# A kernel whose instructions are queued by a 12,085-letter string: the same letters in another order

## The chip, the cores and the metric

The kernel runs on one core of a Trainium2 chip. A core has five instruction queues that run side by side, each in its own order: TensorE (PE, matrix products; the loading of its weights is shown apart as PEld), VectorE (DVE), ScalarE (ACT), GpSimd (POOL) and SyncE (SP, which here only starts DMA transfers). Work on one queue waits for work on another through semaphores. The metric is the device time of one execution in microseconds (us); lower is better.

## The reference, cut to what matters

The input is x, 8 images of 56 x 56 positions with 128 channels, all in float32. Two layers follow one another.

```
# layer 0, per image
xp     = x @ w_in + b_in
h      = gelu(batchnorm(depthwise_conv3x3(x)))
offset = h @ w_off + b_off                   # 4 groups x 9 points x 2
mask   = softmax(h @ w_msk + b_msk)          # over the 9 points
y      = sum over points of mask * bilinear(xp at point + offset) @ w_out + b_out
x      = x + gamma1 * layernorm(y)
x      = x + gamma2 * layernorm(gelu(x @ w_fc1 + b_fc1) @ w_fc2 + b_fc2)
# layer 1, t = x as 3136 tokens per image
n      = layernorm(t)
q, k, v = n @ Wq, n @ Wk, n @ Wv
t      = t + softmax(causal(q @ k.T / sqrt(3136))) @ v
probs  = softmax(layernorm(t) @ gate_w.T + gate_b, over tokens)
# each of 64 experts takes its 8 likeliest tokens of each image,
# pools them by probs, applies a two-layer gelu network,
# and adds the result back to those tokens, weighted by probs
```

## The kernel before, in words

An image is cut into four groups of 448 or 896 tokens (image 0: 448, 896, 896, 896; the others: 896, 896, 896, 448), 32 groups (b, s) in all; a group is worked in tiles of 128 tokens. The bilinear sampling is done as 25 fixed taps around each position: the weights of the taps are computed from the offsets and the mask, a 5 x 5 neighbourhood of each token is gathered from DRAM, multiplied by the weights and added up.

The work of a group is split over twenty Python generators. Each has a letter:

| letter | generator, line | what one group does there | steps in the string |
|---|---|---|---|
| b, k | bring, back | start the loads of x, and of x turned channel-first (xT), on SP | 54, 56 |
| p | prepare L509 | turn x on PE, multiply by w_in (L538), copy into xg, whose edge columns POOL clears (L495), and store the image for the gather | 280 |
| v | conv L562 | depthwise conv, DVE (L576), and its gelu, ACT | 560 |
| c | plan L590 | offsets and mask on PE (L601); softmax and tap weights on DVE (L621, L645, L648), ACT and POOL (L653 to L669) | 912 |
| f | fetch L680 | start the gather of g, 1600 KB per tile, on SP (L691) | 200 |
| g | weigh L696 | copy the weights (ACT, L706), multiply g by them (DVE, L715, 3.5 us a tile) | 256 |
| s | sums L723 | fold the 25 taps on POOL (L732; the first fold of a tile takes 3.5 us), the rest on PE (L747, L749) | 1475 |
| m | project | w_out, layernorm, fc1 (PE L856), gelu (ACT L863), fc2 (PE L877), layernorm | 1432 |
| n | norm L957 | layernorm, and q, k, v on PE | 800 |
| q | scores | q times k on PE (L1066) | 776 |
| x | maxes | scores to SBUF with the row maximum, DVE (L1092, L1108) | 972 |
| e | exps | exp, ACT (L1140) | 776 |
| t, u | turn, pour | transpose the weights on PE (L1158), copy them out of PSUM on ACT (L1173) | 776, 776 |
| a | attend | weights times v on PE (L1203) | 776 |
| y | mix | divide by the row sum and add to t, DVE (L1235) | 102 |
| o | after L1250 | layernorm, gate, and per pair of images the choice of the top 8 tokens (DVE L1344 to L1404, POOL gathers) | 1008 |
| h, w | share L1495, settle | pooling for the experts; derived weights | 82, 16 |

A generator yields before each instruction or small bundle of instructions; up to the next yield is one step. The order in which the steps of all generators are issued is not planned while the kernel is built: it is written out as the string `ORDER` (lines 109 to 242), and the main loop (about line 1754) goes through it letter by letter:

```python
with tc.manual_schedule(engines=engines):
    for line in ORDER:
        if lines["project"].at == len(groups) and not experts:
            give_up()
        lines[NAMES[line]].step()
```

Each letter takes its generator one step on. So the order within a generator is fixed, and the string decides how the twenty are interleaved; that sets the order of the instructions in each of the five queues. An instruction whose data are late holds up everything behind it in its queue. In what follows a step is named by letter, group and count: c(6,1).13 is the fourteenth step of plan for image 6, group 1.

Buffers limit how far one generator may run ahead of another. `rings` counts them: five PSUM banks for general use ("gen"), three gather buffers g, eight score rows S, three q, two xT, two z, one accumulator av. A step that takes a buffer is only written where the string has already given one back. Line 1617 (`class Line`) holds the step; the rules on which group may begin stand from line 1665 on, for instance that project of group n needs sums of group n to be done and after of group n - 4.

ACT holds one table of functions at a time, and changes between gelu and exp need a table load. The load stands where the string puts a gelu step behind an exp step or the other way round.

When the string is used up, a fixed phase for the experts follows (about lines 1765 to 2085); it is the same in both kernels.

Of the kernel before, what the change touches and what calls it, by code (L numbers as in the profile page):

```python
# [79 lines left out]
def need(engine, us, take=None, give=None, since=None, kind=None, when=None, lock=False, also=None):  # L80
# [29 lines left out]
    "ppppbpppppppwbpwwpppwvvfvvvvvvvvbppwcpccccckpwcccpccpccpbpppwfccwvccvccvccvvvccvwwcccvfvcgvg"  # L110
    "vvvvvwvvswsvvgsvcpcccfccspcbppcsppgccccwpcpwcscppvgcsvcvvvvvvcccvfwcvsccbcvcvsvvcvcvscvscsfk"
    "wmvvgvmmmcgcmpbcsfsgpmcvscmccvvcpvsmcsgmsvsmvmvmmmscvcbsmfmpmgfmgmcvsfscgmmmmmmmsnnfnsppnnpn"
    "gccnnsngncnnvnnvsnsvccnqsscvxscfcvpqfcppcevcvxqvscxevcvcqevcksxbpctcecctcmppucmumcpagtpcmgpa"
    "mmuapctbuycgfcpmccbacpmpmscyvoscmcmvmossmmmmcccvcmmsmgmmfvmmsmmsvmvgmommscvmomvcgcmsovscmmmv"
    "fgvmmsfmvmmsovmfovmvvccmomsvgmvmmmmmoosvmncconnsnvpspcnnopnnosogfncskccnnncnsoopnpkponnncpcs"
    "ncgnsnnmcnmgpqqmncxpxmqfsfmxpmnnqmcmgcmmmcxmccmmvmmmxmmmssnmvngvxmmmqnmmqcmsvxxeeqbmxxcmsvee"
    "mmtuvmqmevvqcaxcxvstfxmmgqcmmvvmvuvmmtcvcmcmsxetcbumqgmvufsavtssxmmgcxmmsvqueqmemmnnxcanoste"
    "auqecvtnaunnnsxatfesnngnunncnyqtsnsvunanxxntenqfsaxeouocgcnxstgusqtfnengvkxnaxspuefqssxsstqs"
    "etpemmasnuamqpusftgxxmsqansmxqxpstsassqmuafengeempxusxmysmsqvmvmsmnvatxevssnuvfmqgnsgtxmssaa"
    "vmsmmuvytssugxssmqvtmxtmakaemmmcmmusceesumcmmsssqcesqocqxmxfssstaxkmbauomtssvmtvumqmmcsaxgqu"  # L120
    "mfaqetcxxoaeutecusctqvgsscxsvaumxsqvsaefocqvcosmmvmsxvxmoommtuscsxqtavmqessovmuxsxetmqesemxc"
    "taoumvasqtsymuqmfmcvuxccxapsetnsnxaqetxmcuqcpvatvqmexxxcotcvumanenceotevqnucmxuncvapcbncecpe"
    "ommupepncapqmmpamcgxctnvvpmvvocfpcmmvumomngmsttsnpnsgacmcmnupaqcoxtmbqsmsxeqpmxuucnccxmosacn"
    "oanskntstuapommncsmspsnpesmmsnunmestapgocmucaecpnontsoycsummpnsfoaqqexoqxnomacecncmmoxmssmto"
    "mqstgmmsouxqumqotmfoxgmxmmubxseqoeoxnqsaacgasscepyonteooqutesoousskqotccesuafoomtxqcxxcmxmoo"
    "mmqmmtuoomxooaaxsusqoaatexeosqoeusttesonucosqseqogxxxaukeatvutqxqunatcstxucfxsnsvgssscooaoeu"
    "ennnsaqqasxxtaqsutnexastueoovvsqesqecsfxngutxoqxfoattavxussqqsguesauteevutasuntasxqonsoexqns"
    "smeytsveuaxuctxsqgacmqnuxsqamstnxxmxaeussfmmssssveeaetngmnfqstumamvmssamsvxmuensnmqmtggsxqqm"
    "acnxsfmexssmmtoesstusmsscmgmsnnuqsxmsatmuuatscccqnvuxqanxmfqxnsmemsnemsnecxavcttmsmguvsqcqas"
    "xeantmktbexsmuvvnasuamccuvsneaotevmufvsmmcmvtqusssfacsxmvcgmtmpsmcmqucscsmxqspqscxcqspamaxxe"  # L130
    "mesfctepemmmquxtsectqutxymxeaeeesmuuamctepcqasqtcumcssmaxxqumcgmptutakaapnnnnnnnmunnmtexgpmy"
    "onnmupmpoqtatnnmxabuoufvgxmssvecccqxconnayqnonnosmstxetvecosunnauncssoxtgcmcscsusconqosaasxv"
    "ocncossmocnqaoqxxqxxceqooonxxtcoesunqovqoxaooxxsotsoencsoseoyftnoueccvessqccecvvtamouooeuavf"
    "ctocyoxtmoammqmuouoovtommocueqgvmoaxmxxoatqmmmomxccceaevooooqmxquvmmtooquovtoxxvcmmvuvsmcaet"
    "moxmgomsoossmmomovvmkomovugomoqmmssosxomeqsxqsfmcxmmsesammeptmccmxnbnnnnnettacnpsesecumuamnc"
    "cnftpunsceqatugxqmqcyqnxasacpsxnumxsnqstqscuxtnpsensanquagsvmssencsaxxxncemttnuancssvcutmvne"
    "snqvuxcvsqnfcmscnatsmaxmscgqvasxcxqvemeeusgstuvfassnvvxsmmnasgsstvmfytutcqmmauvxqkquvvevmsxx"
    "vssevatucnentamsuegtqbaxvoxtyqvcusxeqqxmoomaaxecsotvpocxtmuoqecsucqooesomfcaxxauoptmessscmqm"
    "umptgoofeonoatcssuusoopcanatcsxpneoconqnqupvxnxsgotsxaaoesevccspusvtqasuegacteonqsqnuxtcofnx"
    "nuaqsnssofsosevvvnmtxtsxvbgomqubuamsxoxssmqxeaomsqmxtomeummpsmcatsgesssuqsvqevmxqmssepxscyms"  # L140
    "mmctmmamssvaxqtnmfmpcsgsxqsxnummumtmaeumckcmfmtsessqesacxtcsuacaetpusxqqctuneoagxqamscpuasxg"
    "txqpnueqcxtmxetecpumscueaastmfoxstseqceemfmstcpxasqumcosmmumxaguqqqxmcstmsxxxsmteqcmucxessaa"
    "ussstgcqxcecqstfmauxeaeemccycsqmugctxpsssmcacoqustgcaxqccuxmtquasmtcsmmxsxqpmmuseaskeaatexcq"
    "synsoootfcnsooepoonsqutexaopnotuupxsqavoxqetosseuocnnnnunmomxmtssfgqoaquoxsnxanxtsecbqavnteu"
    "oqscexvevutoataamsstvuoeefauvqxegvnoqcqsxxmcutvmasomxussmqtnsnucaoboascmvfvxqvsgtxvmxoesusga"
    "oqmxsomstfemvogmovtosumqsmexmconnussqoemtvsqcessxskasuatsnxmmnxanmxugefasstxnunasxmvmnmmqsex"
    "sovmxemsnmsmtvsnqcutfnsecunamagqxmemsvcxamyssvmmmccccstmsmgsctmsungmsmsmqmqtmecuxcssqefcaxxm"
    "cmtutamugxemcamsqsmkcuteayeqxmuyeysoooposnstooeucmnntnaxsocmspxnooaoononquapocooncxeynpnotco"
    "sfmcqtncuamtnmnxeuoonnacnmnsncmocsunnfkxnsonongoomqmmoaqqnnxeomoxtoqnsoomogpmmunxoonmxooqpmm"
    "sqxmopcstxecsoxcpestqbmoomecxmpuaaqxoucyestsmammtaefmoqmyxempqsouutxvocxmmeoqoumvcaxoeetmqaa"  # L150
    "svoxvutcovsmkomxoscsvsmovtmumoqvogumssomtomvamvgvuvoqmxvoommfxvqaoeoomtxamovmkquosssmaevxssa"
    "vexmxstveesomsqutomqvmvtmcnfoanossnumoxnnxtnqgnoucumcmnospmyqacmxoxponnsnnmsspmsmgspnasxcmte"
    "nuennapqeocoovcmsxactcvuqtqtxsvufsqeavnxcnxsuatcvxcenavnscvsuecnntvfenqscuvsssgsmetssmcnamcv"
    "tuxmmvubavaqceastcqfxqystvucmsgoexvexqvxvussxtmmmsnsvctsaugnmaunaqvvnxeaescyqmtvtmosbusxmucp"
    "qqpoooopomaoetexmqkufpcxnstexoxuqqtcoeastxxavnnunsoaeaupqgxpcnceoscsqaxotpponutgsoevusoqosec"
    "oxnnpnafsxceenvscctuaovocosnotbsvoavouqnstqutagxuopsvxeeovqfsxsqqssvsxxvctaexotupopqsaaegesq"
    "usscmcxmtqutacgxsmestacsumsxtsseqxuqxmcntumcqsscxsmymccmqmmanxceuemtefaqasssmtcmxbsmcsuugmof"
    "txmmqspexmoqesmcsaaxsgctueeusmnpsstgsnmqmaxqmmtasasuxsfsaumsxmgtekumeqteastqmxumtuxsqxaeucss"
    "ssammetamqasfueqmmqgcxctmaqxxmxtseuscueesmctcfucsaotccqeupxxeamqxmsyqsssmxttmmgsatomqcfuqque"
    "xcxaxmxatmcgskemqtmbcuauasemascscmcemnncttesxnuunnqnsunspnynogaqeqosspteaoasuoxtnncfnqtenxsx"  # L160
    "xqxqucaxtsaxosecussnmusenftmaqsbgxsosmenausstspcnsmnspeauqpommtuqetnmnasexmogsnoumxomnvmcnno"
    "ofntqmnqoumtvcxveqxnqnsvsssvaxocvccmtxmauvxfessgssoeemvauctqsvumsmtvcxvvamamssuaemvcvvmeqmmt"
    "tmmsufumcogqmocxmsxaqevoccmmossaxmmoeomcamsgmtuktuomcxmsxmsvvssvovoxmtmqoxuxpaomsspgcoqoxoee"
    "xfsaqsassoppqextpxmystqsesutxmeeqauamsutgmsmtuamsuqmamxtmnesynysqcxocxenynosnoonugtnxanqsxsc"
    "ssuqxaeoaetftsxpteoueuuftnpnssnycmngnomaanftaucxnagumpssnncnmesnnpncononncnspcntemgosqqumqot"
    "cocaxmxsxosocyxnuscmnqoasccxqmmqscvxeasxvxqcvqofsseteoeyumvqexsvsmxomcmmvomstmauoovxtuetoabc"
    "mvckqaxuteacqbgcmmvxovcqocooqusscxmaoetmxstsmmsxumqxfemquvesmexvttmssscuauxavtqmscoxccvsqext"
    "akmmuxevctmauqeomqxqeueoyamsvmxmmgsmvmmmmsmssmmfvmxogmxoootaqvavtmmmxcmuoctsunnasenoooeentsu"
    "nqsnmmoogfnqsoeaopmxxmsoastuqmucsntsmocnasxsmpmgoaxnmmsfmmusnocsnnomoctnnmsnntoomausssugmssn"
    "fmcommmsaanymcpncepnnnsmqgcmnnqmntecmqxmqsuetsxaunsngqoxxtxsuqaaectsxesxcqxebcstufssqssceuac"  # L170
    "ytsoqetqusnaoxeuoxtooxoxaquoosetqkcgautefpuqxaesxtcxeokqcoovoaaqustoxxnoeuxqsvoscoxtvsoauseo"
    "cetttoevnafovuessgtquaaxtvvsneuvauqcqxvxqxqxoooxsqavostunavaoesqsvxcscuvoetssassceesveofcsvm"
    "xutvttcmycquuvaqmocmvgvqxmxmvnaqmugasxncfsmpmncxptpxmemeqtspgpummusscpcpmsmmgemeqscxfemsmcpm"
    "txqavapsvccuscmtsxanuvtmcsusqqmmmbpmscemmasftxxqvsxssmtegenquaaaxtscueqsgnmunvatsasxxuceecvs"
    "tnsmtsuonemccuasmcmvvasvmtmctfqsvquugqssxbpaxxaxcppqpqxeeastutuexyqnemqsfomscetsacxsconqssgm"
    "mmumkmcamsstxpxtqfqgxaxxeumsmctuqkecsaxmmpcutaamemtsmupsybqpoeotecsopoosoconaunosqeccnnenuoq"
    "xtcsuneapnvxsgqtxstvsqxfuovtoqocaxqxooocxaneuaetaxqvetustusugsoosssemnxmanooesouogoeaqcttsav"
    "qvxbaxusquxvnntcvmnmanqfseuqxnoctumoxxmsoseqsatecnfasnvqncunnexessgatqsncuxtsqceexunxsacnsme"
    "smmvnxasctmsstnxcsfugmcuvxnmsxqoavvvsxcavqxsvsmmgtooesvsxcsfoqtscuasvnxqtenseeguvumcsmvtscsa"
# [2675 lines left out]
```

## Time and profile before

| | before |
|---|---|
| median of 3 runs | 2655.1 us |
| lowest, highest | 2653.77, 2659.27 us |
| the profiled execution's own time | 2656.84 us |
| its span from first to last instruction | 2655.0 us |
| mean granted clock of TensorE over the span | 0.972 |
| gathers of g | 192 of 1600 KB, 8 of 800 KB |
| read from and written to HBM | 386.04 and 53.48 MB |

The span is the time between the first and the last recorded instruction of one execution; the 1.84 us between it and the execution's time lie outside. The page gives each engine's busy time as a share of that span. Engines are named PE, PEld, DVE, ACT, POOL and SP; L1066 is line 1066 of the kernel; a pair like "sc<-zT,qT" gives the tile written and the tiles read. The granted clock is the share of full speed at which TensorE was let run. An entry "PE sc L1066 <- DVE S L1092" in the list of waits says that PE, ahead of the instruction of line 1066, stood still for the result that DVE produced at line 1092.

### The profile page before, as it was taken

What the parts mean: (1) busy time and instruction counts of PE and PEld (TensorE: products, weight loads), DVE (VectorE), ACT (ScalarE), POOL (GpSimd) and SP (SyncE); (2) the same over time, 40 slices, a digit from 0 to 9 for tenths busy, and PEclk for the clock granted to TensorE, in tenths of its full rate; (3) what the DMA queues carried; (4) which work ended last, traced back from release to release, by engine and by line L of the source; (5) the groups of instructions that cost most, each with busy time, mean ns of one, the idle gap of its engine ahead of it and who ended that gap; (6) DMA issues with size and microseconds to landing.
All of it is one profiled execution on the core that took longest, in us unless ns stands there. A gap on an engine that the chain in (4) does not pass through costs nothing. (4 is left out here: it accounts for less than half of the span.)

```text
span 2655.0 us, 47647 instructions
## 1 busy us (share of the span) xinstructions
PE 2472.8 (93%) x16297; PEld 1887.9 (71%) x16297; DVE 2164.0 (82%) x4659; ACT 1948.4 (73%) x4532; POOL 2180.2 (82%) x2315
## 2 busy tenths in 40 slices
PE   3799999999999999999999899999999999999974
PEld 3677877777776778777776667767777777777743
DVE  6888877899898987888889897888889988865662
ACT  2356787888787887888778677977888887876631
POOL 3686889889998899989899899987998899882244
PEclk8799999999999999999999999999999999999987
DMA  5665544544554454545454354544465445325083
GB/s 159 204 214 205 208 163 161 198 128 158 189 190 125 160 194 173 175 150 167 169 183 151 122 198 170 181 149 148 162 201 171 145 166 192 136 88 197 23 276 119
DMA packets 274416, 442.63 MB, mean 167 GB/s; under 512 B 14452, under 2 KB 127476, under 8 KB 274164
## 3 DMA queue, kind: packets, MB, share of 16 engines
q1 hardware_dynamic: 184340, 382.09, 41.4%
q10 hardware_dynamic: 86464, 50.94, 6.3%
q0 software_dynamic: 3360, 6.45, 0.8%
q8 instruction: 132, 2.16, 0.4%
q14 instruction: 120, 0.98, 0.1%
HBM read 386.04 MB, written 53.48 MB: 166 GB/s over the span
## 5 line engine op out<-in xcount | busy, mean ns | idle before, releaser
L732 POOL TENSOR_TENSOR g<-g 128x128 f32<-128x128 f32 (+6 forms) x1075 | 1420.9, 1331 | 105.6 <-DVE g L715 25.4
L715 DVE TENSOR_TENSOR g<-g,tp 128x3200 f32<-128x3200 f32 (+1 forms) x200 | 695.0, 3477 | 18.3 <-ACT tp L706 15.9
L1203 PEld LDWEIGHTS av<-v,pe 128*128 128x128 f32 (+2 forms) x5200 | 627.6, 188 | 97.3 <-issue 60.9
L1203 PE MATMUL av<-v,pe 128*128 128x129 f32 (+2 forms) x5200 | 682.7, 277 | 2.8 <-ACT pe L1173 1.6
L1066 PE MATMUL sc<-zT,qT 128*128 128x384 f32 (+8 forms) x1622 | 656.9, 516 | 17.1 <-DVE S L1092 9.9
L1092 DVE TENSOR_SCALAR_CACHE_REDUCE S<-sc 128x512 f32<-128x512 f32 (+5 forms) x783 | 443.3, 576 | 210.1 <-PE sc L1066 124.7
L1140 ACT ACTIVATE S<-S,low 128x512 f32<-128x512 f32 (+5 forms) x783 | 478.8, 638 | 41.9 <-DVE low L1108 30.1
L1173 ACT COPY pe<-tr 128x512 f32<-128x512 f32 (+3 forms) x775 | 380.2, 501 | 144.2 <-PE tr L1158 110.5
L1158 PE MATMUL tr<-ident,S 128*128 128x128 f32 x2516 | 392.3, 276 | 12.6 <-DVE S L1092 9.5
L1158 PEld LDWEIGHTS tr<-ident,S 128*128 128x128 f32 x2516 | 297.0, 142 | 130.7 <-issue 67.0
L1066 PEld LDWEIGHTS sc<-zT,qT 128*128 128x128 f32 (+1 forms) x1622 | 246.6, 187 | 114.1 <-issue 43.3
L576 DVE SCALAR_TENSOR_TENSOR pv<-xg,dw,pv 128x448 f32<-128x448 f32 x448 | 305.7, 682 | 14.2 <-ACT pv L573 8.4
L877 PEld LDWEIGHTS pm<-fc,hid 128*128 128x128 f32 x1600 | 200.4, 193 | 37.6 <-issue 22.6
L877 PE MATMUL pm<-fc,hid 128*128 128x128 f32 x1600 | 222.2, 282 | 1.8 <-POOL hid L862 1.3
L856 PE MATMUL ph<-xT,fc 128*128 128x512 f32 (+2 forms) x448 | 207.3, 551 | 5.2 <-DVE xT L803 3.2
L863 ACT ACTIVATE hid<-ph,b_fc 128x512 f32<-128x512 f32 (+2 forms) x224 | 140.8, 634 | 95.8 <-PE ph L856 92.8
L667 POOL TENSOR_TENSOR taps<-taps,a 128x252 f32<-128x252 f32 (+1 forms) x288 | 191.9, 666 | 8.8
L657 POOL TENSOR_TENSOR a<-w 128x756 f32<-128x756 f32 (+1 forms) x96 | 136.5, 1422 | 20.9 <-DVE w L648 18.4
L760 ACT COPY ys<-ptg 128x128 f32<-128x128 f32 (+1 forms) x200 | 52.6, 263 | 89.4 <-PE ptg L749 47.5
L1140 ACT ACT_TABLE_LOAD x87 | 111.6, 1283 | 4.6 <-DVE pv L576 2.3
L749 PE MATMUL ptg<-ident,g 128*128 128x128 f32 (+1 forms) x650 | 92.0, 307 | 21.7 <-POOL g L732 21.6
L749 PEld LDWEIGHTS ptg<-ident,g 128*128 128x128 f32 (+1 forms) x650 | 88.6, 221 | 25.5 <-POOL g L732 23.7
(328 smaller groups left out, 3712.8 us busy)
## 6 DMA issues: line engine op xcount, KB each, us to landing
g<-img SPq DMA_DIRECT2D x192, 1600.0 KB
w1t<-in_L_ffn_weight_dram SPq DMA_DIRECT2D x32, 512.0 KB
w2t<-in_L_ffn_weight_dram SPq DMA_DIRECT2D x32, 512.0 KB
xin<-in_x_dram SPq DMA_DIRECT2D x56, 224.0 KB
xTd<-xc ACTq DMA_DIRECT2D x56, 224.0 KB
img<-st ACTq DMA_DIRECT2D x112, 112.0 KB
out_dram<-t ACTq DMA_DIRECT2D x24, 448.0 KB
g<-img SPq DMA_DIRECT2D x8, 800.0 KB
```

Of the source, the lines that this page charges most:

```text
L576: nc.vector.scalar_tensor_tensor(p3, src, dw[:, k : k + 1], p3, op0=ALU.mult, op1=ALU.add)
L667: nc.gpsimd.tensor_add(dst, dst, a5[:, :nt, kx])
L715: nc.vector.tensor_mul(g3, g3, tp[:n, lt % 4].unsqueeze(2).to_broadcast([n, NTAP * NG, 32]))
L732: nc.gpsimd.tensor_add(g[:n, o * C : (o + w) * C], g[:n, o * C : (o + w) * C], g[:n, i * C : (i + w) * C])
L856: nc.tensor.matmul(ph[:, :n], fc1[:, f * P : (f + 1) * P], xT[:, :n], start=True, stop=True)
L877: nc.tensor.matmul(four(pm, m)[:, i, :], h[:, i * P : (i + 1) * P], fc2[:, f, :], start=False, stop=i == m - 1 and f == 3,)
L1066: nc.tensor.matmul(pp[h * HALF : h * HALF + qw, c0 : c0 + m], qT[:, q0 : q0 + qw], zTs[b, g][:, k0 : k0 + m], start=True, stop=not seg.las ...
L1092: nc.vector.tensor_scalar(S[p0:p1, c0:c1], pp[p0:p1, c0:c1], -SCALE, None, ALU.mult, ALU.min, accum_out=(mn[p0:p1, i, j + k : j + k + 1] i ...
L1140: nc.scalar.activation(S[p0:p1, c0:c1], S[p0:p1, c0:c1], AF.Exp, bias=low[p0:p1, i : i + 1], scale=-1.0)
L1158: nc.tensor.transpose(pt[:m, k + p0 : k + w], S[p0:w, k : k + m], ident[p0:w, p0:w])
L1173: nc.scalar.copy(pe[:, : full * P], pt[:, : full * P])
L1203: nc.tensor.matmul(p3[h * HALF : h * HALF + qw, i % 3, :], pe[:kw, k + h * HALF : k + h * HALF + qw], vs[b, g][:kw, (k0 + k - c0) // P, :] ...
```

## The change

The 132 lines of the string are replaced. The new string has the same 12,085 letters, each as often as before; the first 12 and the last 5 stand where they stood. Nothing else differs: no instruction is added, removed or resized by the diff itself, apart from the table loads on ACT, whose number follows from the order.

```diff
 ORDER = (
-    "ppppbpppppppwbpwwpppwvvfvvvvvvvvbppwcpccccckpwcccpccpccpbpppwfccwvccvccvccvvvccvwwcccvfvcgvg"
-    "vvvvvwvvswsvvgsvcpcccfccspcbppcsppgccccwpcpwcscppvgcsvcvvvvvvcccvfwcvsccbcvcvsvvcvcvscvscsfk"
...
+    "ppppbppppppppbwwpwppvwvvvvvvvvvbpwcccpccpcpwcccffcpcpcccpppwpvccvcvcvvccccvvwcccccgvvgvbvvsv"
+    "svsvvkvwvvvgpccfwbcfccwppccspcccppcgsppccwscccwpswgbpccsvsvcvccfccvsvvcsvvcvvwvvffvvvccvvvcc"
...
 )
```

The letters move by about 8 places on average; single b and k steps, which only start loads, move by up to some 350. Counted along one queue, with each step's duration taken from the trace of before, the work that stands ahead of a step changes by 1.23 us on average on PE, 1.11 on ACT, 1.10 on DVE and 0.97 on POOL, to either side, and by more than 2 us for 16 to 20% of the steps; the mean over all steps is close to zero. As an example, this is the order of DVE around 1488 us into the span, before and after, each step with its duration in the trace of before:

| before, DVE's queue | after, DVE's queue |
|---|---|
| o(3,3).31, 3.68 us | c(5,1).14, 0.93 us |
| c(5,1).14, 0.93 us | o(3,3).31, 3.68 us |
| o(3,3).32, 4.12 us | o(3,3).32, 4.12 us |
| v(5,2).1, 0.69 us | o(3,3).35, 0.29 us |
| o(3,3).35, 0.29 us | x(4,1).22, 0.55 us |
| y(4,1).0, 1.07 us | x(4,1).23, 0.69 us |
| o(3,3).36, 0.66 us | o(3,3).36, 0.66 us |
| x(4,1).22, 0.55 us | y(4,1).0, 1.07 us |

The change between gelu and exp on ACT occurs 195 times in the string of before and 199 times in the new one.

## The prediction

> **What bounds the kernel now.** I read the windows first, because the change touches only the stretch that the string orders; then the page's busy times and clock; then what PE waits for; then the timeline at the longest waits; last the spread of the DVE steps seen there.
>
> Busy time by stage (columns: window, then busy us and count of PE, PEld, DVE, ACT, POOL, granted clock, DMA share, GB/s): the head, the middle, the fixed expert phase with the string's last steps, and three pieces of the middle.
>
> ```profile
> 0.00:210.00 210.00, 143.97 (x883) 124.96 (x884) 169.38 (x258) 83.86 (x200) 129.65 (x172) 0.84 0.60 197
> 210.00:2540.00 2330.00, 2264.24 (x14589) 1720.15 (x14587) 1945.07 (x4276) 1842.29 (x4272) 1997.22 (x2087) 0.99 0.48 162
> 2540.00:2655.00 115.00, 64.57 (x829) 42.77 (x828) 49.51 (x126) 22.24 (x61) 53.33 (x57) 0.76 0.56 197
> 1250.00:1300.00 50.00, 46.08 (x287) 35.43 (x286) 39.55 (x77) 40.07 (x90) 38.20 (x40) 0.97 0.38 134
> 1450.00:1500.00 50.00, 40.97 (x239) 30.42 (x238) 44.33 (x79) 30.47 (x73) 42.99 (x43) 0.94 0.37 112
> 1800.00:1850.00 50.00, 46.53 (x287) 36.13 (x286) 42.06 (x76) 33.27 (x70) 35.42 (x38) 0.93 0.36 122
> ```
>
> In the middle PE is busy 97%: only 65.8 us (2330 - 2264.24) are idle, against 66.0 in the 210 us of the head and 50.4 in the 115 us of the end. The page's lines of PE and its clock, slice by slice, say the same, and its row of table loads prices a switch between gelu and exp:
>
> ```profile
> PE   3799999999999999999999899999999999999974
> PEclk8799999999999999999999999999999999999987
> L1140 ACT ACT_TABLE_LOAD x87 | 111.6, 1283 | 4.6 <-DVE pv L576 2.3
> ```
>
> What PE waits for in the middle (columns: the pair, us in total, times, longest):
>
> ```profile
> PE sc L1066 <- DVE S L1092: 9.9, 11, 3.1
> PE tr L1158 <- DVE S L1092: 9.5, 8, 4.7
> PE ptg L747 <- POOL g L732: 4.0, 6, 1.2
> PE pq L538 <- POOL xg L495: 3.9, 1, 3.9
> ```
>
> No wait is large by itself. Of the gaps, 56 are of 0.25 us or more, 57.3 us together. The three longest, in the timeline (start, us, engine, line; in brackets the idle before and its releaser):
>
> ```profile
> 1273.37 5.32 POOL L732 TENSOR_TENSOR g<-g 128x1536 f32<-128x1536 f32 x2 [2.42 <-PE po L601]
> 1278.62 0.14 POOL L495 MEMSET xg<- 128x36 f32 x1
> 1278.82 1.73 PE L538 MATMUL pq<-w_in,xg 128*114 128x128 f32 x8 [3.92 <-POOL xg L495]
> ...
> 1488.24 4.12 DVE L1404 TENSOR_SCALAR slot_f<-at_f 32x8 f32<-32x8 f32 x4
> 1495.51 1.11 PE L1158 MATMUL tr<-ident,S 128*128 128x128 f32 x4 [4.67 <-DVE S L1092]
> ...
> 1826.26 5.38 POOL L732 TENSOR_TENSOR g<-g 128x1536 f32<-128x1536 f32 x2
> 1827.20 2.77 DVE L645 TENSOR_TENSOR om<-om,red 128x252 f32<-128x252 f32 x1
> 1830.00 2.43 DVE L648 TENSOR_TENSOR w<-w,om 128x756 f32<-128x756 f32 x1
> 1833.10 1.65 PE L1066 MATMUL sc<-zT,qT 128*128 128x384 f32 x2 [3.07 <-DVE S L1092]
> ```
>
> The reader is to see three causes: a 0.14 us clear queued behind 5.32 us of folds; row maxima queued behind the expert choice (L1404); and row maxima behind two DVE steps that ran long while POOL folded. The spread of the step in the third (least, median and greatest ns):
>
> ```profile
> L645 DVE TENSOR_TENSOR om<-om,red x32: 298/421/3454, 39.5 to 2293.7; 128x252 f32<-128x252 f32 x24, 128x144 f32<-128x144 f32 x8
> ```
>
> Each such wait also costs clock. PE's records show six spells at half rate in the middle, at 832, 849, 1279, 1494, 1515 and 1832 us, four of 3.41 us and two of 6.83, all at waits; half of the 27.3 us, 13.7, is lost.
>
> **The change part by part.** The profiled execution took 2656.84 us (span 2655.0 and 1.84 around it), 1.74 above the median 2655.1. I sum against it.
>
> *Removed and added work: table loads.* The string switches between gelu and exp 199 times instead of 195: 4 x 1.283 = 5.1 us on ACT. ACT is idle for 488 us of the middle (2330 - 1842.29), which hides it; I take 0, with ends 0 and 5.1, should every load land on a chain that PE waits for.
> The Trainium skill (ScalarE: Activation LUTs, What ACT_TABLE_LOAD costs) puts a switch at 1283 ns plus a drain of about 1380, 2.66 us, which would make the four 10.6 us. In the trace the next ACT instruction starts 12 ns after the load (median), so the row stands.
>
> *Moved: the waits that the trace shows.* Of the 57.3 us, 35.4 can be traced to a step that was late. For each I compared two things between the strings: the measured work ahead of the late step on its own engine, and that ahead of the waiting step on PE. Where the first shrinks against the second the wait shrinks as much, down to zero; where it grows the wait deepens. The sum over the traced waits is 21.4 us gone and 15.2 us added. Of the three shown, the one at 1279 loses 2.83 us (the clear of xg(5,0) now stands ahead of both folds) and the one at 1833 loses 1.64 (PE's own queue is longer there). The rest of the relief is in many waits of 1 us or so. Deepened most: c(2,0).0 at 536 us by 3.6, then q(1,2).27 and m(6,2).37. Ends: -21.4 if the deepening is covered, +15.2 if the relief only uncovers another late step.
>
> *Moved: the clock.* With the wait at 1279 its spell of 3.41 us goes: -1.7. Ends 0 and -13.7, all six gone.
>
> *Moved: waits that can't be traced to a step, 21.9 us.* The 4.67 us at 1495 are among them; there the row maxima x(4,1).22 and .23 move ahead of v(5,2).1, y(4,1).0 and o(3,3).36, 2.4 us of DVE. If all fare like the traced (21.4/35.4 = 60%), 13 go. Ends 0 and 21.9.
>
> *Added: waits that the trace of before does not have.* For every step on which PE depends I took by how much more it is delayed than PE's own queue. The largest in each 100 us of the middle add up to 33.2 us; part is eaten by slack, so the ends are 0 and 33.2. I take 13, the same as the untraced relief: these are waits whose place one order has and the other lacks, and nothing in the count says which fits better.
>
> *Moved: DVE against POOL.* The steps at L621, L645 and L648 come 32 times each and stretch when they run beside a fold; over their least duration they lose 83 us in all (23.5, 27.4 and 32.0). Summing over all 96 the POOL step that stands last ahead of each in the string gives 129.9 us before and 139.0 after, 7% more; on 83 us that would be 5.8 of DVE. DVE idles 385 us of the middle, so I take 0, ends +5.8 and -5.8.
> The Trainium skill (SBUF — State Buffer, SBUF: two separate sides) speaks against the change here: DVE with two SBUF inputs and GpSimd share a port pair that whoever starts first holds for its whole instruction, the other blocked. The greatest 3454 ns beside a fold of 3460 agrees. By that rule a hit depends on start times, which the string does not fix, and the 1.64 us at 1833 need not be won: 2648.8 instead of 2647.2.
>
> *Moved: loads on SP.* In PE work between request and use, gathers stand 9.8 us ahead on average (9.2 before), x 36.7 (34.0), xT 21.8 (27.4, least 0.8 against 0.0). The list of waits has no DVE wait on a gather, and three gather buffers bound how early one can start. Taken at 0; without that cover a late load shows as a head wait does: DVE's longest on weights is 4.5 us.
>
> *Head.* DVE bounds it (47.8 of 50 us in 100 to 150), and both strings have the same DVE work before the first project step. The fold s(0,0).9 comes earlier, the taps c(0,1).23 to .28 end where they did, the copy behind them too. 0, ends -4.5 and +4.5 (that longest wait).
>
> *End.* The last group's chain stands in the same order in both; the sharing steps on POOL come slightly later. 0, ends -2 and +2.
>
> Sum: 2656.84 - 21.4 + 15.2 - 1.7 - 13 + 13 = 2648.9; less 1.74, 2647.2 on the median.
>
> **The rivals.**
>
> *No gain (R1).* The new waits are as large as all relief: 20.9 us instead of 13 (13 + 6.2 + 1.7), giving 2655.1. For it: neither order stands out when each is laid on one smooth pace, and a wait seen in one execution is the kind that any reshuffle removes and another replaces. Against: the moves at 1279 and 1495 are plain in the queues.
>
> *Slower: DVE is held at more folds (R2).* Two of the stretched steps with row maxima behind them cost 3.07 us of wait and 1.7 to 3.4 of clock at 1833: 4.8 to 6.5, say 5.5. One or two extra hits (8 us of gain at 5.5) undo the forecast; four put it at 2647 + 22 = 2669. For it: the 139.0 against 129.9, and c(6,1).13 and .14 still stand just ahead of a first fold of s(6,0) while another POOL step, 1.26 us, is put before it. Against: DVE's 385 idle us, and in before only 11 hits of over 2 us among the 96 steps, few of which PE felt.
>
> *Much faster (R3).* The relief holds, the deepening and the new waits vanish in slack, the untraced go by 13 and half the clock loss with them: 2656.84 - 21.4 - 13 - 6.9 = 2615.5, less 1.74 is 2614; with half the 13 of new waits, 2620. Against: it asks that only favourable moves act.
>
> **How the numbers follow.** The measurement tells 0.2% (5.3 us) from no change: faster is below 2649.8, slower above 2660.4. The forecast's own case has 0.40 (own range 2636 to 2653, so 0.34 faster, 0.06 same), R1 0.18 (0.02 faster, 0.11 same, 0.05 slower), R2 0.30 (slower), R3 0.12 (faster). Sums: faster 0.48, same 0.17, slower 0.35. The range 2626 to 2671 leaves out most of R3 (about 0.09) and the part of R2 with more than four hits or with all 33.2 us of new waits (about 0.11); the bounds of the small terms (5.1, 5.8, 4.5, 2) lie inside it.
>
> **What would show it.** Right: the wait of L538 on L495 is gone and the piece around 1279 has no half-rate spell; the waits of L1066 and L1158 on L1092 sum to less than 19.4; PE's idle time in the middle is below 65.8, about 59; table loads number four more. R2 shows as greater medians of L645 and L648 and more waits on L1092; R1 as PE idle unchanged with other pairs in the list. I am wrong altogether if the time moves in the head or the end, or if a load becomes what DVE waits for.

## The result and the profile after

The new order is slower. The median is 2663.17 us over 8 runs (2660.71 to 2667.67), against 2655.47 for the kernel before over 8 runs (2653.59 to 2659.27): a ratio of 1.0030, 95% interval 1.0021 to 1.0039, so 7.7 us more. The forecast was 2647.2, so the miss is 16 us.

The profiled execution has a span of 2660.8 us, 5.8 more than before. First the windows by stage, the same stretches as those shown of before (window, then busy us and count of PE, PEld, DVE, ACT, POOL, granted clock, DMA share, GB/s):

```profile
0.00:210.00 210.00, 141.72 (x926) 121.78 (x927) 174.49 (x263) 90.01 (x213) 132.53 (x174) 0.89 0.64 210
210.00:2540.00 2330.00, 2255.96 (x14475) 1714.32 (x14475) 1947.03 (x4264) 1836.48 (x4256) 1992.51 (x2080) 0.99 0.47 161
1250.00:1300.00 50.00, 49.49 (x318) 37.38 (x317) 43.40 (x84) 43.91 (x96) 44.05 (x46) 1.00 0.47 169
1450.00:1500.00 50.00, 38.66 (x240) 28.97 (x238) 48.21 (x78) 31.99 (x76) 48.33 (x48) 0.97 0.33 104
1800.00:1850.00 50.00, 49.01 (x319) 38.05 (x318) 45.12 (x82) 39.19 (x83) 41.65 (x41) 1.00 0.48 172
```

The head issues more matmuls in the same 210 us (926 against 883) at a better clock. The pieces around 1279 and 1833, where the forecast saw waits go, are full now: PE busy 49.5 and 49.0 of 50 us, clock 1.00. The piece around 1495 is worse: PE is busy for 38.7 of its 50 us instead of 41.0. But in the whole middle PE is idle for 74.0 us (2330 - 2255.96) instead of 65.8. The list of what PE waits for there shows other pairs on top:

```profile
PE ph L856 <- DVE S L1092: 9.8, 3, 8.2
PE tr L1158 <- DVE S L1092: 8.2, 7, 2.5
PE ph L856 <- DVE xT L803: 6.5, 7, 1.9
PE sc L1066 <- DVE S L1092: 5.5, 8, 1.8
PE pq L538 <- POOL xg L495: 5.1, 1, 5.1
PE tr L1158 <- DVE om L609: 3.8, 2, 3.6
```

To see where the time goes, every matmul of PE was matched with its twin in the other trace (the n-th of its line, since a generator's order is fixed), and its end after minus its end before taken. The median of this lag over some 20 us from each named time, by the twin's time in the trace of before (negative: earlier than before; the length of the stretch moves single rows by up to about 1 us):

| at, us | lag, us | what changed since the row above |
|---|---|---|
| 250 | -7.5 | the head |
| 640 | -5.6 | |
| 660 | +0.9 | one wait, at 646 |
| 720 | -0.2 | |
| 760 | +7.7 | one wait, at 733, and its sequel |
| 1200 | +9.0 | |
| 1300 | +4.1 | the wait at 1279 of before is gone |
| 1500 | +6.6 | |
| 1600 | +3.1 | |
| 1800 | +2.0 | |
| 1850 | -3.7 | the wait at 1833 of before is gone |
| 2300 | +5.3 | small steps |
| 2600 | +5.8 | |

So the two orders run neck and neck with a few jumps. Nothing happens in the end phase. Two jumps, 6.5 and about 8 us, stand out among the losses; 9 us more go in small steps between 1850 and 2300 us.

The first jump, in the timeline of the new order (start, us, engine, line; in brackets the idle before and its releaser):

```profile
643.28 3.47 POOL L732 TENSOR_TENSOR g<-g 128x1536 f32<-128x1536 f32 x1
646.70 1.68 POOL L669 TENSOR_TENSOR taps<-taps,inside 128x700 f32<-128x700 f32 x1
648.33 2.88 POOL L732 TENSOR_TENSOR g<-g 128x768 f32<-128x768 f32 x2
651.14 0.15 POOL L495 MEMSET xg<- 128x36 f32 x1
651.34 2.05 PE L538 MATMUL pq<-w_in,xg 128*114 128x128 f32 x8 [5.08 <-POOL xg L495]
```

It is the fault that the prediction saw removed at 1279, with another tile: the 0.15 us clear of xg(3,0) is queued behind 8 us of folds and taps, PE waits 5.08 us and then multiplies at half rate, for 6.83 us by its clock records. In the trace of before the same clear stands ahead of the long fold and the taps:

```profile
649.84 0.15 POOL L495 MEMSET xg<- 128x36 f32 x1
650.15 3.48 POOL L732 TENSOR_TENSOR g<-g 128x1536 f32<-128x1536 f32 x1
```

The second jump:

```profile
729.82 6.18 DVE L1315 TENSOR_SCALAR ci<-cu 64x8 f32<-64x8 uint32 x1
730.51 1.67 POOL L669 TENSOR_TENSOR taps<-taps,inside 128x700 f32<-128x700 f32 x1
732.14 5.72 POOL L732 TENSOR_TENSOR g<-g 128x128 f32<-128x128 f32 x3
736.03 0.61 DVE L609 TENSOR_TENSOR om<-po,b_om 128x432 f32<-128x432 f32 x1
736.69 1.12 PE L1158 MATMUL tr<-ident,S 128*128 128x128 f32 x4 [3.59 <-DVE om L609]
```

A DVE instruction on 64 x 8 values took 6.18 us while POOL worked without a pause; DVE's next step, which empties a PSUM bank, and with it PE stood behind it. The spread of that line, of the new order and then of the order before (least, median, greatest ns):

```profile
L1315 DVE TENSOR_SCALAR ci<-cu x31: 162/492/6177, 284.8 to 2528.4; 64x8 f32<-64x8 uint32 x31
```

```profile
L1315 DVE TENSOR_SCALAR ci<-cu x31: 162/311/3354, 272.8 to 2521.4; 64x8 f32<-64x8 uint32 x31
```

### The profile page after: what moved, and what is told of

It is laid out like the page before. It is cut to its first block, busy times and chain, and to the rows that moved or that the text cites. A ratio compares the mean times of both kernels' runs of the same rounds, so it can differ in the third digit from the quotient of the medians.

```text
span 2660.8 us, 47650 instructions
## 1 busy us (share of the span) xinstructions
PE 2468.1 (93%) x16297; PEld 1883.8 (71%) x16297; DVE 2173.6 (82%) x4659; ACT 1951.7 (73%) x4536; POOL 2182.7 (82%) x2315
## 5 line engine op out<-in xcount | busy, mean ns | idle before, releaser
L732 POOL TENSOR_TENSOR g<-g 128x128 f32<-128x128 f32 (+6 forms) x1075 | 1422.4, 1332 | 95.1 <-DVE g L715 21.7
L1066 PE MATMUL sc<-zT,qT 128*128 128x384 f32 (+8 forms) x1622 | 657.7, 516 | 13.5 <-DVE S L1092 5.5
L1092 DVE TENSOR_SCALAR_CACHE_REDUCE S<-sc 128x512 f32<-128x512 f32 (+5 forms) x783 | 442.9, 577 | 209.6 <-PE sc L1066 143.8
L1158 PE MATMUL tr<-ident,S 128*128 128x128 f32 x2516 | 393.1, 276 | 18.4 <-DVE S L1092 8.2
L1158 PEld LDWEIGHTS tr<-ident,S 128*128 128x128 f32 x2516 | 297.4, 142 | 134.9 <-issue 61.3
L1066 PEld LDWEIGHTS sc<-zT,qT 128*128 128x128 f32 (+1 forms) x1622 | 248.5, 187 | 104.7 <-issue 44.5
L877 PEld LDWEIGHTS pm<-fc,hid 128*128 128x128 f32 x1600 | 200.4, 193 | 39.4 <-issue 22.6
L856 PE MATMUL ph<-xT,fc 128*128 128x512 f32 (+2 forms) x448 | 208.2, 552 | 18.5 <-DVE S L1092 9.8
L877 PE MATMUL pm<-fc,hid 128*128 128x128 f32 x1600 | 222.0, 281 | 3.1 <-POOL hid L862 1.8
L667 POOL TENSOR_TENSOR taps<-taps,a 128x252 f32<-128x252 f32 (+1 forms) x288 | 191.6, 665 | 8.4
L749 PE MATMUL ptg<-ident,g 128*128 128x128 f32 (+1 forms) x650 | 85.0, 292 | 35.6 <-POOL g L732 35.6
L749 PEld LDWEIGHTS ptg<-ident,g 128*128 128x128 f32 (+1 forms) x650 | 81.9, 207 | 39.2 <-POOL g L732 38.2
```

The source lines that it names most:

```text
L667: nc.gpsimd.tensor_add(dst, dst, a5[:, :nt, kx])
L732: nc.gpsimd.tensor_add(g[:n, o * C : (o + w) * C], g[:n, o * C : (o + w) * C], g[:n, i * C : (i + w) * C])
L856: nc.tensor.matmul(ph[:, :n], fc1[:, f * P : (f + 1) * P], xT[:, :n], start=True, stop=True)
L877: nc.tensor.matmul(four(pm, m)[:, i, :], h[:, i * P : (i + 1) * P], fc2[:, f, :], start=False, stop=i == m - 1 and f == 3,)
L1066: nc.tensor.matmul(pp[h * HALF : h * HALF + qw, c0 : c0 + m], qT[:, q0 : q0 + qw], zTs[b, g][:, k0 : k0 + m], start=True, stop=not seg.las ...
L1092: nc.vector.tensor_scalar(S[p0:p1, c0:c1], pp[p0:p1, c0:c1], -SCALE, None, ALU.mult, ALU.min, accum_out=(mn[p0:p1, i, j + k : j + k + 1] i ...
```

## The experiments

**Theory A**: each jump belongs to its place in the string, because PE's queue is full on both sides of it; the loss is the two places named, and the head is a gain. **The rivals**: the lateness is diffuse, so that PE merely stops at the next late step when one is mended; or a gain is given back further on. Ratios are to the kernel before, run on the same chip alongside. Three chips were used. On one, called the first here, the kernel before takes 2655 us, as in the main comparison; on the two slower ones 2696 to 2698. In the traces of these two PE waits 15 to 16 us at L1835 of the expert phase, where those of the first chip have 1.8 to 1.9. The kernel before was traced on a chip of 2655 us alone. PE's lag against that trace can be compared across chips up to about 2400 us; behind that the slower chips lose time that the first does not, as will be seen. Times are compared only as ratios.

**The head alone.** Both strings have issued exactly the same steps after 504 letters, so the heads can be exchanged.

```diff
-ORDER = before
+ORDER = after[:504] + before[504:]
```

> The order of before, with its first 504 letters (the first 200 us, after which both orders have issued exactly the same steps) replaced by those of the new order. Theory A (the loss sits in a few places of the middle, and the new head is a gain that they hide): the steps after the head come 6.8 us earlier in the trace of the new order, and nothing behind it changes, so 2655.5 - 6.8 = about 2648.7. Rival B (lateness spreads evenly and the starting point of the middle decides nothing, or the head's gain is given back at the first wait): about 2655. Rival C (the middle's new waits follow from its earlier start, not from its order): about 2663.

Measured, on a slower chip: ratio 0.9978, interval 0.9969 to 0.9987, some 6 us. In its trace PE is 7.9 us early at 250 us and at 1200 us still 8.3. So the head's gain is real and the middle's losses do not follow from it. But by 2300 us only 3.2 us of it are left, although the letters there are those of before. Among what is new in its trace are a wait of 1.97 us for POOL at 1518 us (L877 on L862, 0.65 before) and a hold of DVE (L1315 at 1555.55 us takes 2.38 us, in the trace of before 0.35). Part of a gain is thus given back, as the second rival says. Where it comes from, on ACT, before and then after:

```profile
97.38 0.21 ACT L760 COPY ys<-ptg 128x64 f32<-128x64 f32 x1 [9.46 <-PE ptg L749]
97.49 0.50 ACT L706 COPY tp<-taps 128x400 f32<-128x400 f32 x1
```

```profile
93.18 0.21 ACT L760 COPY ys<-ptg 128x64 f32<-128x64 f32 x1 [5.66 <-PE ptg L749]
93.77 0.50 ACT L706 COPY tp<-taps 128x400 f32<-128x400 f32 x1 [0.37 <-POOL taps L669]
```

The copy of the weights tp, for which DVE waited 4.5 us, stands in ACT's queue behind a copy that waits for PE, and PE waits for the fold s(0,0).9. The new order issues that fold before the last taps (83.87 instead of 88.06 us).

**The clear.** The steps of the new order around it, with the edit:

```diff
 m(1,3).23
+p(3,0).0
+p(3,0).1
 s(2,0).40
...
 s(2,0).41
 u(1,2).5
-p(3,0).0
...
 s(2,0).42
 o(1,1).11
-p(3,0).1
```

> The new order with the two steps p(3,0).0 and .1 put ahead of the fold s(2,0).40, so that the clear of xg(3,0) that p(3,0).1 issues on POOL stands ahead of three folds and the taps. Theory A: the wait of L538 on L495 of 5.1 us at 646 us goes, with 1.7 us of clock: 2663.2 - 6.7 = about 2656.5. Rival B (PE stops at the next late step instead): 2661 to 2664.

**The held instruction.**

```diff
-        nc.vector.tensor_scalar_add(ci[:, k8], cu[half_], float((b % 2) * T + first(b, s)))
+        at_pool = nc.gpsimd if (b, s) == (1, 1) else nc.vector
+        at_pool.tensor_scalar_add(ci[:, k8], cu[half_], float((b % 2) * T + first(b, s)))
```

> The new order, with the one instruction of L1315 of group (1,1) (64 x 8 values, 6.18 us in the trace of the new order, least 0.16) moved from DVE to POOL; all else as it was. Theory A: DVE is held there by POOL's folds, the wait of 3.6 us at 733 us and what follows it go: 2663.2 - 6 to 8 = about 2656. Rival B (the next DVE step with operands in SBUF is held in its place): 2661 to 2664.

**Both edits**, the two diffs above together.

> Both edits of the two runs ahead of this one. Theory A: 2663.2 - 6.7 - 7 = about 2649.5, faster than before by about 6; the two places carry the whole loss. Rival B: above 2660.

Measured, all three on a slower chip: the clear 1.0033 (1.0020 to 1.0047), the held instruction 1.0024 (1.0013 to 1.0034), both 1.0008 (0.9998 to 1.0018). By their times the first two are about where rival B put them (2661 to 2664 is 1.0021 to 1.0032), and both together bring less than half of what theory A expected (0.0022 of 0.0053). The traces say why. Lag of PE against the trace of before:

| at, us | new order | clear moved | L1315 moved | both |
|---|---|---|---|---|
| 640 | -5.6 | -5.4 | -4.0 | -5.4 |
| 660 | +0.9 | -5.9 | +1.7 | -5.9 |
| 720 | -0.2 | -6.1 | -0.1 | -6.7 |
| 760 | +7.7 | +1.6 | +2.3 | -3.9 |
| 1200 | +9.0 | -0.4 | +1.7 | -3.0 |
| 1850 | -3.7 | -11.6 | -10.8 | -14.4 |
| 2300 | +5.3 | +0.2 | -1.7 | -2.3 |

At the place itself the first edit takes away its jump and the second 5.5 of its 7.9 us (with L1315 alone PE then still waits 2.2 us for the tap weights, L747 on L653), and nothing of it returns at the next late step: at 1200 us both together are 12.0 us ahead of the new order. The POOL queue with the clear moved (both edits):

```profile
644.00 0.15 POOL L495 MEMSET xg<- 128x36 f32 x1
644.21 0.15 POOL L497 MEMSET xg<- 128x58 f32 x1
644.31 3.46 POOL L732 TENSOR_TENSOR g<-g 128x1536 f32<-128x1536 f32 x1
```

Later some is lost. In the two kernels with the clear moved, DVE is held once more at L1315, where the new order has 0.42 us and the kernel with L1315 alone 0.46 (the line is from the kernel with the clear alone; in that with both it took 2.71 us):

```profile
2116.63 2.69 DVE L1315 TENSOR_SCALAR ci<-cu 64x8 f32<-64x8 uint32 x1
```

There both lose 3.3 to 3.6 us between 2110 and 2120 us, the kernel with L1315 alone 1.0. It seems that a move at 646 us shifted the meeting of DVE and POOL at 2115 us; there is one trace of each. All three share the new order's slow loss between 1850 and 2300 us. And from 2400 to 2540 us each falls back by another 12.7 to 13.0 us, the kernel with the head alone, on the same chip, by 5.9, and the new order on the first chip by 0.3. There ACT stands still for up to 6.2 us, for a releaser that the profile of this core doesn't show; what it is stays open. So these three times can't settle what the two places cost; the runs on the first chip, which follow, can.

**That loss too.** The new order with both edits, and with the order of before from about 1855 to 2388 us (where the strings match exactly again). At cuts where they match only nearly, here and in the runs below, the 5 to 50 letters behind the cut (155 at one cut of the finer choice) are arranged anew, so that each step still comes once:

```diff
-ORDER = after
+ORDER = after with p(3,0).0 and .1 moved, and before's order from letter 8669 to 11400
...
+        at_pool = nc.gpsimd if (b, s) == (1, 1) else nc.vector
```

> The new order with both edits (the clear of xg(3,0) ahead of the folds, L1315 of group (1,1) on POOL) and with the order of before from about 1855 to 2388 us, where the trace of the new order loses 9 us in small steps. Theory A: 2663.2 - 11.7 - 9 = 2642.5, a ratio to before of 0.995. Rival B (the small steps are chance, and any order loses them there): 1.000 or above.

Measured, on the first chip: 2640.8 us beside 2655.21, ratio 0.9942 (0.9928 to 0.9955), 22.4 us below the new order where 20.7 were expected. PE's lag is -2.5 at 1200, so the two places return 11.5 us on this chip too; it is -12.4 at 1850 and -12.5 at 2300, and stays there. So the small steps belong to the order of that stretch. Two of the three largest waits in it, in the trace of the new order:

```profile
1960.37 2.28 DVE L1315 TENSOR_SCALAR ci<-cu 64x8 f32<-64x8 uint32 x1
1963.44 1.13 PE L1066 MATMUL sc<-zT,qT 128*128 128x512 f32 x2 [1.77 <-DVE S L1092]
...
2038.84 3.45 DVE L715 TENSOR_TENSOR g<-g,tp 128x3200 f32<-128x3200 f32 x1
2043.90 0.63 PE L1158 MATMUL tr<-ident,S 128*128 128x128 f32 x4 [2.50 <-DVE S L1092]
```

One is L1315 held again; in the other, row maxima stand behind a full multiplication of g. The remaining waits are of 1 to 2 us or below what the list shows.

**The loss put into the order of before.** One stretch of the new order, from about 580 to 770 us, in the order of before:

```diff
-ORDER = before
+ORDER = before with after's order in letters 2300 to 3254
```

> The order of before with one stretch from the new order, at about 580 to 770 us, which holds both the clear of xg(3,0) behind the folds and the instruction of L1315 that was held for 6.18 us. Theory A: the trace of the new order loses 11.7 us there against before, so a ratio of 1.0044. Rival B (the two waits came from where the new order entered the stretch): 1.000.

Measured, on the first chip: 2669.36, ratio 1.0054 (1.0040 to 1.0067), 14.2 us; lag -0.7 at 600 and +11.9 at 760 us. The list of waits between 600 and 800 us is that of the new order:

```profile
PE pq L538 <- POOL xg L495: 5.1, 1, 5.1
PE tr L1158 <- DVE om L609: 3.9, 2, 3.6
```

**The clear of before.** The same edit for xg(5,0), in the order of before:

```diff
+p(5,0).0
+p(5,0).1
 s(4,1).0
...
 s(4,1).1
 m(4,0).7
-p(5,0).0
...
 x(3,2).30
-p(5,0).1
 t(3,2).19
```

> The order of before with p(5,0).0 and .1 ahead of the fold s(4,1).0, so that the clear of xg(5,0) stands ahead of two folds. Theory A: the wait of 3.92 us at 1279 us goes, with its spell of half clock; the new order, which has this, gains 4.1 us there: ratio 0.998. Rival B (PE stops at the next late step): 1.000.

Measured, on the first chip: 0.9989 (0.9980 to 0.9998), and a lag that falls from -1.8 at 1240 to -6.1 at 1300 us. The step has the expected size; the time shows 2.7 us of it, between the two expectations.

**The gains without the losses.** The order of before with four stretches of the new one:

```diff
-ORDER = before
+ORDER = before with after's order in letters 0 to 504, 5602 to 5976, 7131 to 7641 and 8274 to 8669
```

> The order of before with four stretches from the new order: the first 504 letters, and the stretches that lie at about 1230 to 1307, 1543 to 1651 and 1772 to 1855 us, in which the trace of the new order gains on that of before by 5.1, 4.5 and 8.5 us. Theory A (each stretch's gain belongs to the stretch, because PE's queue is full at both of its ends): 7.9 + 5.1 + 4.5 + 8.5 = 26 us less than before, a ratio of 0.990. Rival B (what a stretch gains depends on how the queues enter it, and most is given back): a ratio of 0.995 to 1.000.

Measured, on the first chip: 2633.5 us, ratio 0.9915 (0.9902 to 0.9929), 21.7 us faster than before and 29.7 faster than the new order. The lag is -7.0 after the head, -12.9 at 1300, -16.7 at 1600, -23.8 at 1850, and stays there.

**A finer choice of stretches.**

```diff
-ORDER = before
+ORDER = before with after's order in letters 0 to 930, 3513 to 3722, 5312 to 6088 and 7131 to 8669
```

> The order of before with the stretches of the new order chosen over all near-matching points of the two strings by the lag of PE between the two traces: the head to 312 us, 821 to 865, 1172 to 1332 and 1543 to 1855 us. Their gains in the traces add up to 29 us. Theory A (gains belong to their stretch): a ratio to before of 0.989 to 0.990. Rival B (choosing by one trace of each picks chance differences, which do not return): no better than 0.9915, what four coarser stretches gave.

Measured, on a slower chip: 0.9924 (0.9911 to 0.9938). Its lag at 1850 is -25.7, so the stretches gave what they promised up to there but for 3 us; the time is no better than with the coarse choice, as rival B said. But 6 us of the lag go between 2400 and 2540 us, where the coarse choice, on the first chip, lost 1.2. Which choice is better is not shown.

**Taking the held instructions from DVE.** In the order of before, L1315 and L1404 on POOL:

```diff
-        nc.vector.tensor_scalar_add(ci[:, k8], cu[half_], float((b % 2) * T + first(b, s)))
+        nc.gpsimd.tensor_scalar_add(ci[:, k8], cu[half_], float((b % 2) * T + first(b, s)))
...
-                nc.vector.tensor_scalar_add(
+                nc.gpsimd.tensor_scalar_add(
                     slot_f[r : r + 32, g, h], at_f[src, p], float((p % 2) * 2 * T)
```

> The order of before, unchanged, with the small DVE instructions of L1315 (64 x 8, 31 of them) and L1404 (32 x 8, 16 of them) issued on POOL instead. Theory A (DVE is held there while POOL folds, and row maxima stand behind): the 20.0 and 5.9 us that these lines lose over their least duration leave DVE, and the wait of L1158 of 4.67 us at 1495 us shrinks with its clock: 4 to 8 us less, a ratio of 0.997 to 0.9985. Rival B (DVE's idle time hides the stretch, or the next DVE step is held instead): 1.000. Rival C (47 more instructions delay POOL's folds): above 1.000.

Measured, on a slower chip: 1.0118 (1.0101 to 1.0135), some 32 us slower: rival C, by another mechanism than it named. On POOL one of these takes 0.24 us, but it waits for the search on DVE in front of it, and the folds wait behind it. The waits of POOL in the list:

```profile
POOL ci L1315 <- DVE cu L1314: 66.4, 23, 11.7
```

The same two edits of the code with the finer choice of stretches:

```diff
-ORDER = before
+ORDER = before with after's order in letters 0 to 930, 3513 to 3722, 5312 to 6088 and 7131 to 8669
...
-        nc.vector.tensor_scalar_add(ci[:, k8], cu[half_], float((b % 2) * T + first(b, s)))
+        nc.gpsimd.tensor_scalar_add(ci[:, k8], cu[half_], float((b % 2) * T + first(b, s)))
...
-                nc.vector.tensor_scalar_add(
+                nc.gpsimd.tensor_scalar_add(
```

> The two runs ahead of this one together. Theory A: the gains add up, a ratio of about 0.987. Rival B: that of the better of the two.

Measured, on the same chip: 1.0020 (1.0008 to 1.0031). It loses nearly as much against the finer choice (1.0020 to 0.9924) as the run before lost against before. What moving does well is seen in one place only: between 1475 and 1500 us the lag of the kernel with both lines on POOL falls by 5.2 us, from 21.0 to 15.8. There L1404, whose operands are long ready, no longer holds DVE. So, last, L1404 alone, with the four stretches:

```diff
-ORDER = before
+ORDER = before with after's order in letters 0 to 504, 5602 to 5976, 7131 to 7641 and 8274 to 8669
...
-                nc.vector.tensor_scalar_add(
+                nc.gpsimd.tensor_scalar_add(
                     slot_f[r : r + 32, g, h], at_f[src, p], float((p % 2) * 2 * T)
```

> The order of before with the four stretches of the new order (0 to 200, 1230 to 1307, 1543 to 1651 and 1772 to 1855 us), and with L1404 alone (32 x 8, 16 of them, their operands long ready) issued on POOL. In the run that moved both small lines the stretch around 1495 us became 5.2 us shorter, while POOL stood 66.4 us waiting for DVE at L1315. Theory A (L1404 was held by POOL's folds, and on POOL it waits for nothing): the 4.67 us wait at 1495 us and its half clock go, 4 to 5 us less than the 0.9915 of the same order: 0.9895 to 0.990. Rival B (another DVE step is held there instead, or POOL waits here too): 0.9915 or above.

Measured, on the other slower chip: 0.9910 (0.9891 to 0.9929), which lies between the two expectations and decides nothing. In the traces the 4.66 us wait of L1158 at 1478 us, still there with the four stretches, is gone, and PE, level with that kernel at 1475 us, is 2.7 us earlier at 1500 and 3.2 at 2000 us.

## Why the prediction was wrong

The sign was wrong: the prediction put too little on waits that only the new order has. By its own steps:

- *Waits that the trace of before shows*: right in the places named, wrong in size. The waits at 1279 and 1833 went, with their half-rate spells (the clock of both pieces is 1.00), 4.9 and 5.7 us in the lag. But matched matmul by matmul, the waits of 0.25 us or more of the middle (60 with 59.5 us by this count, where the prediction has 56 and 57.3) lose 54.2 us, and not the 34.4 of its traced and untraced relief together, and they deepen by 5.1 us and not by 15.2: where the deepest was forecast, at 536 us, 1.42 us became none.
- *Waits that before does not have*: the step that failed. It was set at 13 us, equal to the untraced relief, out of a count that gave 33.2 at most. By the same matching, 53 matmuls that waited less than 0.25 us before wait for 59.8 us now. A wait that merely moves to a neighbouring matmul stands in both sums, so their difference is firmer than either; PE's idle time in the middle shows it, 74.0 us for 65.8, where 59 was forecast. The clear of xg(3,0) was not in the count, since that went by the engine of each step, and this clear is issued on POOL by a step of ACT. Its place can be read from the two queues: the same tile of another image, the same line, again behind folds. The line of the forecast "the wait of L538 on L495 is gone" is false for that reason: 5.1 us in place of 3.9.
- *Untraced waits*: at 1495 the wait did not go, as this sum had hoped. There DVE is now held several times in a row (L645, L648, L1373, and once in L1404), and PE waits at L856:

```profile
1485.57 3.78 DVE L645 TENSOR_TENSOR om<-om,red 128x252 f32<-128x252 f32 x1
1492.79 2.46 DVE L1373 TENSOR_TENSOR cn<-cn,cs 128x4 f32<-128x4 f32 x1
1500.86 1.65 PE L856 MATMUL ph<-xT,fc 128*128 128x384 f32 x2 [8.17 <-DVE S L1092]
```

- *A sign that misled*: the waits of L1066 and L1158 on L1092 did fall below 19.4, to 13.7 us. But L856 now waits for the same line, and all of PE's waits on it are 28.3 us in the middle, 28.1 before.
- *The clock*: -1.7 was forecast. Instead of six spells at half rate in the middle, 27.3 us, there are eight, 37.5 us; by the prediction's reckoning of half, 5.1 us more are lost. With the 8.2 us of idle that is 13.3 us, by which PE falls back between 250 and 2600 us (from -7.5 to +5.8).
- *DVE against POOL*: the mechanism was weighed, but not all of its lines. The count covered L621, L645 and L648, and the sum was taken at 0 with ends of 5.8. The 83 us there are counted over the least duration of the smaller shape; over the least of each shape these three lose 70.3 us before and 78.6 after, 12% more where 7% was forecast. L1315 was in no term: 20.0 us before, 33.3 after, with the 6.18 us at 730. The cover named, DVE's 385 idle us, is no cover where PE waits for the very next DVE step.
- *Head*: taken at 0, measured -7.5 in the lag. The step said that the copy ends where the taps end; the trace of before had it start 3.6 us after them (taps 93.90, copy 97.49), behind a copy that waited for a fold which moves. The end -4.5 was also too near, and time that moves in the head is what the prediction itself called being wrong altogether.
- *Table loads, loads on SP, end*: no loss is seen there. The table loads number 202 instead of 198; DVE's waits on gathers in the middle are 1.1 us, 0.9 before (the prediction saw none); and the lag does not move in the end.
- *R2* had the sign and the right kind of cause. By its measure the hits of over 2 us on its three lines went from 11 to 15, the four more that it feared; but what PE lost is not four times 5.5 us. It is one hold of some 8 us at a line that R2 did not count, one wait that has nothing to do with it, and many small ones. *R1* had the mechanism nearest to the matching, new waits as large as all relief; they were larger.

The sum, 2647.2, comes near what the lag suggests for the order without the two places (2663.2 - 12.0 is 2651), but that is luck: its terms for relief and for new waits were both far too small, and the kernel with both edits measured 1.0008 on a slower chip.

## What to carry to other kernels

Where all queues are nearly full, an order is judged by the waits that it makes, the few worst places first (14 us here, and 9 more in small steps), and not by the mean of its shifts: lay out, for each new order, which short instruction with a waiting consumer stands behind a run of long ones on its own queue, and count side instructions that a step issues on another engine than its own. When two orders pass through the same state at some points, cut them there: the lag of matched instructions shows which stretch of which is better, and the better stretches added up here to 21.7 of the 26 us that they promised. Before an instruction is moved to another engine to free it from a hold, see what it waits for, since everything on the new queue will wait with it.

## What the runs showed of the hardware

A DVE instruction that is held can stay held through several POOL instructions. The 64 x 8 instruction of L1315 began at 729.82 us, while POOL was in a tap instruction (L667) that ended at 730.15. POOL went on back to back with a fold of 0.46 us, taps of 1.67 (L669) and folds of 0.46 and 3.42 until 735.97, and paused 0.08 us before the next fold, which needs the result of the one before; DVE ended at 736.00. The Trainium skill (SBUF — State Buffer, SBUF: two separate sides) has GpSimd, or a DVE instruction of the kinds that it lists, hold the shared port pair for its whole instruction when it starts first, while the other is blocked; read as the rest of one instruction, the hold would have ended at 730.15. The measured end, after the fifth, decides.

A pause of POOL is not needed for the end, though: of the 14 holds of this line over 1 us in the new order, five ended while POOL had gone straight on to its next instruction. One is that at 1960.37 us, over at 1962.65:

```profile
1959.19 3.44 POOL L732 TENSOR_TENSOR g<-g 128x1536 f32<-128x1536 f32 x1
1962.57 0.50 POOL L667 TENSOR_TENSOR taps<-taps,a 128x144 f32<-128x144 f32 x1
```

What lets a hold pass from one POOL instruction to the next is not shown.

These holds are not chance. In other kernels, and on another chip, the same stretch of the string gives the same hold: 6.18 us at 730 in the new order, 6.17 at 724 in that with the clear moved and 6.19 at 734 in the order of before with that stretch; 3.24 to 3.27 at 1200 to 1218 us in the six kernels that have the new order there. But a shift of a few us upstream can make a new one, as at 1555 us in the kernel with the new head and, it seems, at 2115 us.
